# Graph-attention kernel: biases of neighbouring projections as two 32-row products in different row groups, and all bias parts in one tile

## Chip, cores and metric

The kernel runs on one NeuronCore of a Trainium2 chip. The metric is device time in microseconds (us), as the median of the runs; the profile describes one execution, and its span reaches from the first to the last instruction.

## The reference

One pre-norm graph-attention layer with B = 16 batches, N = 1024 nodes, D = 512 channels, and 8 heads of 64 channels, all in fp32. The adjacency matrix is sparse and shared by the batches; a node attends only to the nodes it is linked to.

```python
h = jnp.maximum(_layernorm(x, axis=-1), 0.0)
q = (h @ Wq + bq).reshape(b, n, H, HD)
k = (h @ Wk + bk).reshape(b, n, H, HD)
v = (h @ Wv + bv).reshape(b, n, H, HD)
scores = jnp.einsum('bihd,bjhd->bhij', q, k) / jnp.sqrt(jnp.float32(HD))
scores = scores + jnp.where(adj == 0, -1e9, 0.0)[None, None, :, :]
weights = jax.nn.softmax(scores, axis=-1)
out = x + jnp.einsum('bhij,bjhd->bihd', weights, v).reshape(b, n, H * HD)
```

The setup sets the three bias vectors to zero, but the kernel computes with whatever they hold.

## The kernel before, in words

**Tiles.** The nodes are sorted by degree once, at the start, and each batch is handled as 8 tiles of 128 nodes in that order. For each tile n the kernel loads the rows of x (`load_x`), takes layer-norm statistics on VectorE (`stats`, `variance`, `shift`, with `power` on GpSimd), normalises on ScalarE (`norm`, L644), turns the tile over with four TensorE transposes (`flip`, L651), and copies the result to SBUF on ScalarE (`unflip`, L656). Then come three projections of that tile by TensorE: K and V (`proj_kv`, evicted from PSUM by ScalarE at L672 into `kvt` and stored to a table `kv` in DRAM) and Q (`queries`, which stays in PSUM in tile `pq` until VectorE has multiplied it with the gathered keys at L895).

**One projection.** `project` (L658 to L661) issues five matrix products into one PSUM tile of 128x512. First the bias: a bf16 matrix product of `chosen` (128x128, rows 0, 64 and 96 ones, the rest zeros) with `bias[name]` (128x512, whose rows 0, 64 and 96 hold the bias as a sum of three bf16 parts). Then, for four chunks of 128 input channels, the fp32 product of the turned tile with the weights; each of these four appears as two instructions in the profile, so that a projection is one bias instruction and eight product instructions. There are 384 projections: 128 each of K, V and Q.

**Attention.** A unit is a tile (or a part of one) with up to four neighbours per node. GpSimd gathers rows of K and V from the `kv` table with indirect DMAs (`gather`, L885), VectorE multiplies with q and sums over each head (`multiply` L895, `score` L899), ScalarE takes the exponential and weights V (`exponent` L903, `weigh_s` L921), VectorE and GpSimd add the neighbours up (`fold` L926), and TensorE adds up for the tiles that are not folded fully (`add_up` L944). Output rows leave by indirect DMA (`put_out`, L988). A batch's first gather needs all eight tiles of that batch's K and V in the table, so the projections of the next batch run beside the attention of the present one.

**Order.** Nothing is scheduled by the compiler. `plan_of` lists every step with an engine, an assumed length, a place and what it depends on, and simulates the five engines; the order that comes out is the order in which the steps are written, and each engine takes its own instructions in that order. A projection is planned with 3.70 us (K, V) or 3.66 us (Q). PSUM has two buffers for K and V (`pkv`) and two for Q (`q`).

**Bias at the start.** `load_b` (L514) issues three small DMAs per bias from SyncE, nine in all, one into each of rows 0, 64 and 96 of a zeroed fp32 scratch area, behind the loads of two x tiles and of Wk and ahead of the loads of the other x tiles and of adj. `round` (L518) casts to bf16 on ScalarE, `remain` (L522) subtracts on GpSimd what the cast has kept, and each bias goes through round, remain, round, remain, round: nine casts and six subtractions. A K projection waits only for K's last cast, and so on.

Of the kernel before, what the change touches and what calls it, by code (L numbers as in the profile page):

```python
# [45 lines left out]

UNITS = (
    (7, 0, 2),
    (6, 0, 3),
    (5, 0, 3),  # L50
    (4, 0, 4),
    (3, 0, 3),
    (3, 3, 2),
    (2, 0, 3),
    (2, 3, 3),
    (1, 0, 4),
    (1, 4, 4),
    (0, 0, 4),
    (-1, 0, 4),
    (0, 4, 4),  # L60
    (0, 8, 3),
)
SHARES = (7, 6, 5, 4)
DIRECT = (7, 6, 5, 4, 3, 2, 1)
LAST_ORDER = (10, 11, 12, 13, 8, 9, 6, 7, 4, 5, 3, 2, 1, 0)
LAST_DIRECT = (7,)
POOL_FOLDS = (2, 3, 8, 9, 11)
UMAX = max(n for _, _, n in UNITS)
SLOTS = sum(n for _, _, n in UNITS) + len(CAPS) + 1
NU = len(UNITS)  # L70
NT = len(CAPS)
BY_VECTOR = {2: 1, 3: 0, 4: 1}
ONE_MORE = (6,)
BY_VECTOR_LAST = {2: 1, 3: 1, 4: 1}
# [97 lines left out]
def plan_of(B):  # L172
# [15 lines left out]
    for k, load in enumerate(loads):  # L188
        uses = [("x", load[1])] if load[0] == "load_x" else []
        add(load, "SP", 0.9 if load[0] == "load_b" else 0.2, -90 + k, uses=uses, delay=4.6, moves=size[load[0]])  # L190
    for j in range(3):
        for k, name in enumerate(names):
            place = -70 + 4 * k + j
            add(("round", name, j), "ACT", 0.58, place, [("remain", name, j - 1) if j else ("load_b", name)])
            if j < 2:
                add(("remain", name, j), "POOL", 1.3, place, [("round", name, j)])
    for t in range(NT):
# [40 lines left out]
    for n in range(-NT, tiles):  # L238
        b, j = divmod(n, NT)
        ahead = 0 if n >= 0 else 60 if n < 4 - NT else 19.47 - 1.3 * j  # L240
        p = (b - 1) * NU + j * rate if b > 0 else j * rate - 20.77 if b == 0 else 1.5 * j - 42.92
        if n >= 0:
            known = [("perm_of",)] if b == 0 else []
            add(("load_x", n), "POOL", 1.35, p - 5.47, known, [("x", n)], delay=4.5, moves=0.75)
        if b:
            add(("stats", n), "DVE", 0.84, p - ahead - 4.00, [("load_x", n)], [("x", n)])
        m, k, size = group_of(n)
        if b and k == size - 1:
            add(("variance", m), "DVE", 0.33, p - ahead - 5.38, [("stats", n - k) for k in range(size)])
            add(("power", m), "POOL", 1.1, p - ahead - 4.87, [("variance", m)])  # L250
            add(("shift", m), "DVE", 0.37, p - ahead - 4.29, [("power", m)])
        add(("norm", n), "ACT", 0.76, p - 6.38, [("shift", m) if b else ("load_x", n)], [("x", n), ("h", n)], delay=0.00)
        add(("flip", n), "PE", 0.62, p - 3.43, [("norm", n)], [("h", n), ("pht", n)])
        add(("unflip", n), "ACT", 0.53, p - 2.57, [("flip", n)], [("pht", n), ("hT", n)])
        if b == 0:
            continue
        for w in range(2):
            e = p - -0.51 + 0.3 * w + (1.41 if n < 3 - NT and w else 0.0)
            ready = [("unflip", n)]
            if n < 0:  # L260
                ready += [("round", "kv"[w], 2), ("load_w", "kv"[w])]
            add(("proj_kv", n, w), "PE", 3.70, e, ready, [("hT", n), ("pkv", n, w)])
            add(("evict_kv", n, w), "ACT", 0.53, e - 0.99, [("proj_kv", n, w)], [("pkv", n, w), ("kvt", n)])
        ready = [("evict_kv", n, w) for w in range(2)]
        if n >= 0:
            add(("store_kv", n), "SP", 0.1, p, ready, [("kvt", n)], delay=2.5, moves=1.5)
        else:
            add(("store_kv", n), "POOL", 1.35, p, ready + [("ranks",)] + ([("store_kv", n - 1)] if n > -NT else []), [("kvt", n)], delay=2.5, moves=1.5)
# [3 lines left out]
    for k in range(units):  # L272
# [4 lines left out]
        t, _, count = UNITS[u]  # L277
        n = b * NT + NT - 1 - t
        q = ("q", b, t)
        if q not in q_of:  # L280
            p = i - 2.12
            if t >= 0:
                ready = [("unflip", n)] + ([("round", "q", 2), ("load_w", "q")] if b == 0 else [])
                add(("queries", b, t), "PE", 3.66, p, ready, [("hT", n), q])
                if t == 0:
                    add(("copy_q", b), "ACT", 0.57, p + 0.5, [("queries", b, 0)], [q, ("q0", b)])
            else:
                add(("queries", b, t), "PE", 0.9, p, [("copy_q", b)], [q, ("q0", b)])
# [26 lines left out]
        for n in folds(b, B, t, count):  # L315
            on_pool = n[1] == 1 and u in POOL_FOLDS
            add(("fold", k, *n), "POOL" if on_pool else "DVE", 1.4 if on_pool else 0.45 * n[1] + 0.35, i + 0.90, weighed, [g], delay=1.67 if on_pool else 0.15)
# [14 lines left out]
        if u == parts[-1]:  # L332
            n = b * NT + NT - 1 - home
            by = ("DVE", 0.75) if residual_by_vector(b, B, home) else ("POOL", 1.5)
# [41 lines left out]


def by_vector(b, B, u):

    count = UNITS[u][2]  # L380
    return BY_VECTOR[count] + (u in ONE_MORE) if b < B - 1 else BY_VECTOR_LAST[count]

# [18 lines left out]
def main_path(tc, x, adj, Wq, bq, Wk, bk, Wv, bv, out, sums, cover):  # L401
# [10 lines left out]
    with ExitStack() as ctx:  # L412
# [35 lines left out]
        matrices = dict(k=Wk, v=Wv, q=Wq)  # L448
        rest = {name: scratch[:, 0, ts(k, H * HD)] if k < 2 else scratch[:, 1, : H * HD] for k, name in enumerate(names)}
        nc.gpsimd.memset(scratch[:, 0:2, :], 0.0)  # L450
# [11 lines left out]

        starts = (0, 64, 96)
        chosen = const.tile([P, P], BF16, tag="chosen", name="chosen")
        nc.gpsimd.memset(chosen, 0.0)
        for start in starts:
            nc.gpsimd.memset(chosen[start : start + 1, :], 1.0)
        minus_half = const.tile([P, 1], F32, tag="mhalf", name="minus_half")
# [27 lines left out]
        nc.gpsimd.tensor_copy(before["told"][:, :, own], place)  # L496
        bias = {name: const.tile([P, H * HD], BF16, tag="b" + name, name=f"b{name}_parts") for name in names}

# [15 lines left out]
        def load_b(name):  # L514
            for start in starts:
                nc.sync.dma_start(rest[name][start : start + 1, :], vectors[name].rearrange("(o n) -> o n", o=1))

        def round(name, j):  # L518
            rows = slice(starts[j], P)
            nc.scalar.copy(bias[name][rows, :], rest[name][rows, :])  # L520

        def remain(name, j):  # L522
            rows = slice(starts[j + 1], P)
            nc.gpsimd.tensor_tensor(rest[name][rows, :], rest[name][rows, :], bias[name][rows, :], ALU.subtract)

# [72 lines left out]
        def tile_at(n):  # L598


            return (n // NT, NT - 1 - n % NT) if n >= 0 else ("first", n + NT)

# [54 lines left out]

        def project(pt, name, n):  # L658
            nc.tensor.matmul(pt, chosen, bias[name], start=True, stop=False)  # L659
            for c in range(DC):  # L660
                nc.tensor.matmul(pt, HT[n][:, c, :], W[name][:, c, :], start=False, stop=(c == DC - 1))  # L661

        def proj_kv(n, j):
            b, t = tile_at(n)
            PT[n, j] = ps_kv.tile([P, D], F32, tag="pkv", name=f"p{'kv'[j]}_{b}_{t}")
            project(PT[n, j], "kv"[j], n)

# [199 lines left out]
        def queries(b, t):  # L867
            Q[b, t] = ps_q.tile([P, D], F32, tag="q", name=f"pq_{b}_{t}")
            if t >= 0:
                project(Q[b, t], "q", b * NT + NT - 1 - t)  # L870
            else:
# [51 lines left out]
        def fold(i, first, n):  # L923
            v = G[i][:, :, 1, :]
            engine = nc.gpsimd if n == 1 and i % NU in POOL_FOLDS else nc.vector
            engine.tensor_tensor(v[:, 0:n], v[:, 0:n], v[:, first : first + n], ALU.add)  # L926
# [55 lines left out]
        def residual(b, t):  # L982
            rows = X[b * NT + NT - 1 - t]
            add = G.pop(b * NU + parts_of(t)[0])[:, 0, 1, :] if shares_in(b, B, t) else O.pop((b, t))
            (nc.vector if residual_by_vector(b, B, t) else nc.gpsimd).tensor_tensor(rows, rows, add, ALU.add)  # L985

        def put_out(b, t):
            nc.gpsimd.indirect_dma_start(  # L988
                out=out_rows, out_offset=on(ap=perm[:, t : t + 1], axis=0), in_=X.pop(b * NT + NT - 1 - t)[:], in_offset=None,
                element_offset=b * N * D,  # L990
            )

        do = (
            zeros, load_adj, load_w, load_b, round, remain, degree, no_diagonal, keys, flip_row, copy_row, rank_of, ranks, ends, list_of,
            tell, spread, collect, others, perm_of, spots, long_rows, long_blocks, longest, count_pieces, first_piece, owners, flip_owners, copy_owners, list_pieces, pieces, slots, load_x, stats, variance, power, shift, norm, flip, unflip, proj_kv, evict_kv, store_kv,
# [3 lines left out]
        do = {f.__name__: f for f in do}  # L999
        for name, *args in plan_of(B):  # L1000
            do[name](*args)
# [186 lines left out]
```

## Time and profile before

| what | value |
|---|---|
| median of 3 runs | 1742.09 us (1739.52 to 1748.52) |
| span of the profiled execution | 1721.4 us |
| granted TensorE clock, mean | 0.981 |
| TensorE products, busy | 1601.7 us, 93% of the span, 4295 instructions |
| VectorE, ScalarE, GpSimd, busy | 87%, 86%, 73% of the span |
| mean DMA rate | 309 GB/s |

The profiled execution's own time is known only as its span. The median lies 20.7 us above that span: start and end of the launch, which the profile does not cover, and the difference from run to run. In the lines of the profile, PE is TensorE's products, PEld its weight loads (which run beside products), DVE is VectorE, ACT ScalarE, POOL GpSimd and SP SyncE; an instruction's end on PE is modelled, its start is recorded. A form such as 128*128 is the part of the array used, rows by columns; `128x512 bf16` is the operand. L659 is line 659 of the kernel.

### The profile page before, as it was taken

The numbers are of one execution on the slowest core, as the hardware profiler recorded it, in microseconds if no ns is written. First come the engines' busy times: TensorE is split into PE (matmuls) and PEld (weight loads), VectorE is DVE, ScalarE is ACT, GpSimd is POOL, SyncE is SP. The second block draws the span as 40 slices with busy tenths as digits, with TensorE's granted clock in tenths as the row PEclk, the third lists the DMA queues.
The fourth block names the chain that finished last, engine by engine and source line by source line (L and its number), as shares of the span: only waits on it lengthen the run. The fifth ranks groups of instructions, "written<-read, shape, count | busy, mean of one in ns | idle before, by whom it ended". The sixth has DMA issues, their size and how long they took to land.

```text
span 1721.4 us, 19566 instructions
## 1 busy us (share of the span) xinstructions
PE 1601.7 (93%) x4295; PEld 740.1 (43%) x4295; DVE 1506.2 (87%) x1921; ACT 1479.7 (86%) x5484; POOL 1264.2 (73%) x1161
## 2 busy tenths in 40 slices
PE   6979999999999999999999999999999999999896
PEld 3434444444444444444444444444444444444332
DVE  6789889898989989899998889989888998988896
ACT  5249989898998989899898989989898997979895
POOL 4757777787877778777877778778687777867654
PEclk9989999999999999999999999999999999999998
DMA  6397889899898989989898898889989888988893
GB/s 235 122 319 269 313 309 348 315 336 331 305 327 303 360 309 331 325 306 326 306 358 320 308 338 301 324 311 338 337 317 329 298 318 312 336 329 290 299 356 141
DMA packets 150741, 531.73 MB, mean 309 GB/s; under 512 B 19916, under 2 KB 19916, under 8 KB 150616
## 3 DMA queue, kind: packets, MB, share of 16 engines
q0 software_dynamic: 109840, 390.70, 64.4%
q1 hardware_dynamic: 40776, 139.71, 21.4%
q8 instruction: 36, 0.59, 0.1%
q14 instruction: 89, 0.73, 0.1%
HBM read 429.51 MB, written 100.82 MB: 308 GB/s over the span
## 4 chain that ended last, share of the span: by engine, by line
PE 74%; DMA 9%; DVE 3%; POOL 2%; ACT 1%; issue 1%; DVEq 0%; POOLq 0%; ACTq 0%
PE pv L661 22%; PE pk L661 22%; PE pq L661 20%; DMA g<-kv,index 8%; PE acc L944 3%; DVE g L895 2%; PE pht L651 2%; PE pv L659 1%; PE pk L659 1%; PE pq L659 1%; POOL g L885 1%; DMA kv<-kvt 1%; ACT hT L656 0%; ACT h L644 0%; DMA out_dram<-x,perm 0%
## 5 line engine op out<-in xcount | busy, mean ns | idle before, releaser
L921 ACT ACTIVATE g<-g,weights 128x64 f32<-128x64 f32 x4696 | 1155.8, 338 | 15.1 <-DVE weights L908 14.3
L885 POOL DMA_INDIRECT g<-kv,index x608 | 631.3, 1038 | 225.7 <-issue 144.5
L895 DVE TENSOR_TENSOR g<-g,pq 128x1536 f32<-128x1536 f32 (+2 forms) x208 | 388.1, 1871 | 101.6 <-DMA g<-kv,index 73.7
L661 PE MATMUL pq<-wq,hT 128*128 128x512 f32 x1024 | 470.8, 603 | 0.0
L661 PE MATMUL pk<-wk,hT 128*128 128x512 f32 x960 | 431.5, 592 | 0.0
L661 PE MATMUL pv<-wv,hT 128*128 128x512 f32 x960 | 431.5, 592 | 0.0
L899 DVE TENSOR_REDUCE weights<-g 128x32 f32<-128x2048 f32 (+2 forms) x224 | 424.1, 1893 | 0.6
L661 PEld LDWEIGHTS pq<-wq,hT 128*128 128x128 f32 x1024 | 198.1, 193 | 273.9 <-issue 270.1
L926 DVE TENSOR_TENSOR g<-g 128x512 f32<-128x512 f32 (+1 forms) x301 | 257.7, 860 | 27.6 <-ACT g L921 27.2
L661 PEld LDWEIGHTS pv<-wv,hT 128*128 128x128 f32 x960 | 182.4, 190 | 215.1 <-issue 212.0
L661 PEld LDWEIGHTS pk<-wk,hT 128*128 128x128 f32 x960 | 182.4, 190 | 205.5 <-issue 202.0
L609 POOL DMA_INDIRECT x<-in_x_dram,perm x128 | 148.8, 1162 | 39.9 <-issue 33.6
L988 POOL DMA_INDIRECT out_dram<-x,perm x128 | 133.7, 1045 | 50.9 <-issue 19.9
L926 POOL TENSOR_TENSOR g<-g 128x512 f32<-128x512 f32 x90 | 118.9, 1321 | 67.5 <-DVE g L926 58.6
L915 DVE TENSOR_TENSOR g<-g,weights 128x512 f32<-128x512 f32 x149 | 124.3, 834 | 2.1 <-ACT weights L903 1.8
L644 ACT ACTIVATE h<-x,shift,rstd 128x512 f32<-128x512 f32 x120 | 94.5, 812 | 28.7 <-issue 14.7
L903 ACT ACTIVATE weights<-weights 128x32 f32<-128x32 f32 (+2 forms) x224 | 49.7, 222 | 71.9 <-DVE weights L899 71.8
L985 POOL TENSOR_TENSOR x<-x,o 128x512 f32<-128x512 f32 x67 | 89.3, 1333 | 11.5 <-DVE o L976 7.8
L944 PE MATMUL acc<-g,ident 128*128 128x512 f32 x170 | 86.4, 622 | 9.0 <-DMA g<-kv,index 5.4
L659 PE MATMUL pq<-bq_parts,chosen 128*128 128x512 bf16 x128 | 48.8, 382 | 47.9 <-DVE g L895 47.9
L651 PE MATMUL pht<-ident,h 128*128 128x128 f32 x512 | 73.8, 276 | 18.5 <-ACT hT L656 16.5
L651 PEld LDWEIGHTS pht<-ident,h 128*128 128x128 f32 x512 | 60.6, 142 | 64.7 <-issue 33.9
(231 smaller groups left out, 1147.5 us busy)
## 6 DMA issues: line engine op xcount, KB each, us to landing
g<-kv SPq DMA_DIRECT2D x128, 512.0 KB
kv<-kvt SPq DMA_DIRECT2D x120, 512.0 KB
g<-kv,index POOLq DMA_INDIRECT x608, 6.8
adj<-in_adj_dram SPq DMA_DIRECT2D x8, 512.0 KB
x_first<-in_x_dram SPq DMA_DIRECT2D x8, 256.0 KB
x<-in_x_dram,perm POOLq DMA_INDIRECT x128, 6.3
out_dram<-x,perm POOLq DMA_INDIRECT x128, 5.5
wk<-in_L_gnn_Wk_dram SPq DMA_DIRECT2D x1, 1024.0 KB
```

Of the source, the lines that this page charges most:

```text
L609: nc.gpsimd.indirect_dma_start(out=X[n][:], out_offset=None, in_=x_rows, in_offset=on(ap=perm[:, t : t + 1], axis=0), element_offset=b * N * D
L651: nc.tensor.transpose(PH[n][:, c, :], hn[:, ts(c, P)], ident)
L659: nc.tensor.matmul(pt, chosen, bias[name], start=True, stop=False)
L661: nc.tensor.matmul(pt, HT[n][:, c, :], W[name][:, c, :], start=False, stop=(c == DC - 1))
L885: nc.gpsimd.indirect_dma_start(out=G[i][:, s].rearrange("p j d -> p (j d)"), out_offset=None, in_=KV[b % len(KV)][:], in_offset=on(ap=inde ...
L895: nc.vector.tensor_tensor(k, k, Q[b, t][:, None, :].to_broadcast([P, count, D]), ALU.mult)
L899: nc.vector.tensor_reduce(weights[:, w, :], heads(G[i][:, :count, 0, :]), AX.X, ALU.add)
L915: nc.vector.tensor_tensor(v, v, own.to_broadcast([P, n, H, HD]), ALU.mult)
L921: nc.scalar.activation(v[:, h, :], v[:, h, :], AF.Identity, scale=weights[:, c + s, h : h + 1])
L926: engine.tensor_tensor(v[:, 0:n], v[:, 0:n], v[:, first : first + n], ALU.add)
L944: nc.tensor.matmul(ACC[b, home], owner_t if t < 0 else ident, v[:, s, :], start=(u == parts_of(home)[0] and s == 0), stop=(u == parts_of(h ...
L988: nc.gpsimd.indirect_dma_start(out=out_rows, out_offset=on(ap=perm[:, t : t + 1], axis=0), in_=X.pop(b * NT + NT - 1 - t)[:], in_offset=No ...
```

## The change

It does the following, and leaves the rest of the computation as it is.

- **One bias tile.** The three biases lie in one 128x512 bf16 tile, in four groups of 32 rows, in the order k, v, q, q. The first three rows of a group hold the three parts of its bias, the other 29 are zero.
- **Loading.** Each group is filled by one DMA that writes the vector into three rows: four DMAs in place of nine.
- **Splitting.** `parts_at` makes two columns of ones and zeros on VectorE (rows from which the second and third part count), with two reductions and two small operations. The split then runs once for all biases: three ScalarE steps (the first two with a scale column) and two GpSimd subtractions, over all 128 rows. All projections now wait for the last of these.
- **Products.** `bias_places` goes through TensorE's steps in the planned order. Where two projections follow each other directly, and are not K after K or V after V, they form a pair: the first takes its bias at its end, the second at its beginning, so that the two bias products stand side by side. Each is a 32-row product with all-one weights from another group of 32 rows. A projection without such a neighbour keeps a 128-row bias product at its beginning, with a weight matrix (`chosen_of`) that has ones in its own group's rows.
- **Names.** Units, orders and shares are now named by tile and first neighbour rather than by number (`TILES`, `PARTS`, `LAST_TILES`, `POOL_FOLDS`, `ONE_MORE`). The values come out the same as before.

The core of the diff:

```diff
-            add(("round", name, j), "ACT", 0.58, place, [("remain", name, j - 1) if j else ("load_b", name)])
-            if j < 2:
-                add(("remain", name, j), "POOL", 1.3, place, [("round", name, j)])
+    add(("parts_at",), "DVE", 0.5, -70)
     for j in range(3):
+        known = [("remain", j - 1)] if j else [("parts_at",)] + [("load_b", name) for name in names]
+        add(("round", j), "ACT", 0.58, -70 + j, known)
+        if j < 2:
+            add(("remain", j), "POOL", 1.3, -70 + j, [("round", j)])
...
+def bias_places(order):
+    on_pe = ("proj_kv", "queries", "flip", "add_up", "pass_on", "flip_row", "first_piece", "flip_owners", "list_pieces")
+    ops = [op for op in order if op[0] in on_pe]
+    name = lambda op: None if op[0] not in ("proj_kv", "queries") or op[2] == -1 else "q" if op[0] == "queries" else "kv"[op[2]]
+    at = {}
+    for one, two in zip(ops, ops[1:]):
+        if one in at or name(one) is None or name(two) is None:
+            continue
+        g, h = GROUPS.index(name(one)), GROUPS.index(name(two))
+        if g == h:
+            if GROUPS.count(name(one)) == 1:
+                continue
+            h = GROUPS.index(name(one), g + 1)
+        at[one], at[two] = (False, g), (True, h)
+    return at
...
-        starts = (0, 64, 96)
         chosen = const.tile([P, P], BF16, tag="chosen", name="chosen")
-        nc.gpsimd.memset(chosen, 0.0)
-        for start in starts:
-            nc.gpsimd.memset(chosen[start : start + 1, :], 1.0)
+        nc.gpsimd.memset(chosen, 1.0)
+        chosen_of = const.tile([P, len(names), P], BF16, tag="chosen_of", name="chosen_of")
+        nc.gpsimd.memset(chosen_of, 0.0)
+        for g in range(len(names)):
+            nc.gpsimd.memset(chosen_of[32 * g : 32 * g + 32, g, :], 1.0)
...
         def load_b(name):
-            for start in starts:
-                nc.sync.dma_start(rest[name][start : start + 1, :], vectors[name].rearrange("(o n) -> o n", o=1))
+            vec = vectors[name]
+            rows = bass.AP(tensor=vec.tensor, offset=vec.offset, ap=[[0, 3], [1, H * HD]])
+            for g, owner_name in enumerate(GROUPS):
+                if name == owner_name:
+                    nc.sync.dma_start(rest[32 * g : 32 * g + 3, :], rows)
+
+        def parts_at():
+            ends_at = [once.tile([P, 1], F32, tag=f"ends{j}", name=f"ends_at_{j}") for j in range(2)]
+            for j in range(2):
+                nc.vector.tensor_reduce(ends_at[j], ident.rearrange("p (g r) -> p g r", r=32)[:, :, j], AX.X, ALU.add)
+            nc.vector.tensor_scalar(later[0], ends_at[0], -1.0, 1.0, op0=ALU.mult, op1=ALU.add)
+            nc.vector.tensor_tensor(later[1], later[0], ends_at[1], ALU.subtract)
+
+        def round(j):
+            if j < 2:
+                nc.scalar.activation(part, rest, AF.Identity, scale=later[j])
+            else:
+                nc.scalar.copy(bias, rest)
+
+        def remain(j):
+            nc.gpsimd.tensor_tensor(rest, rest, part, ALU.subtract)
...
-        def project(pt, name, n):
-            nc.tensor.matmul(pt, chosen, bias[name], start=True, stop=False)
+        def project(pt, name, n, op):
+            ahead, g = bias_at.get(op, (True, None))
+            rows = slice(0, P) if g is None else slice(32 * g, 32 * g + 32)
+            ones = chosen_of[:, GROUPS.index(name), :] if g is None else chosen[rows, :]
+            if ahead:
+                nc.tensor.matmul(pt, ones, bias[rows, :], start=True, stop=False)
             for c in range(DC):
-                nc.tensor.matmul(pt, HT[n][:, c, :], W[name][:, c, :], start=False, stop=(c == DC - 1))
+                nc.tensor.matmul(pt, HT[n][:, c, :], W[name][:, c, :], start=(c == 0 and not ahead), stop=(c == DC - 1 and ahead))
+            if not ahead:
+                nc.tensor.matmul(pt, ones, bias[rows, :], start=False, stop=True)
```

## The prediction

> **What bounds the kernel now.** I read first the page's busy times and the shares of the chain that ended last (its engines, then its lines), to see which engine sets the end.
>
> ```profile
> PE 1601.7 (93%) x4295; PEld 740.1 (43%) x4295; DVE 1506.2 (87%) x1921; ACT 1479.7 (86%) x5484; POOL 1264.2 (73%) x1161
> ...
> PE 74%; DMA 9%; DVE 3%; POOL 2%; ACT 1%; issue 1%; DVEq 0%; POOLq 0%; ACTq 0%
> PE pv L661 22%; PE pk L661 22%; PE pq L661 20%; DMA g<-kv,index 8%; PE acc L944 3%; DVE g L895 2%; PE pht L651 2%; PE pv L659 1%; PE pk L659 1%; PE pq L659 1%; POOL g L885 1%; DMA kv<-kvt 1%; ACT hT L656 0%; ACT h L644 0%; DMA out_dram<-x,perm 0%
> ```
>
> TensorE's projections are most of the chain; the bias products (L659) are in it with some 1% for each of pq, pk and pv. The one sizeable other link is the gather, which the list of the chain shows as 8 to 9 us once a batch. A stretch of 100 us, about one batch, says how much room the others have (columns: busy us and count for PE, PEld, DVE, ACT, POOL, then clock, DMA share, GB/s):
>
> ```profile
> 400.00:500.00 100.00, 95.74 (x260) 44.30 (x259) 90.30 (x108) 91.52 (x343) 76.61 (x69) 1.00 0.90 329
> ```
>
> VectorE, ScalarE and the DMA engines have 8 to 10% left, and TensorE nothing but the waits. These are TensorE's two largest in the list of waits (total us, times, longest):
>
> ```profile
> PE pq L659 <- DVE g L895: 47.9, 28, 4.1
> PE pht L651 <- ACT hT L656: 16.5, 17, 1.0
> ```
>
> The first comes twice a batch, where a batch begins: q's PSUM buffers are full until the first gathers land. So a batch is TensorE's row of products plus this fixed gap. The price of a bias product is read in the timeline of PE (start, us, then the instructions merged), and of its weight load in that of PEld:
>
> ```profile
> 833.40 0.38 PE L659 MATMUL pq<-bq_parts,chosen 128*128 128x512 bf16 x1
> 833.62 3.60 PE L661 MATMUL pq<-wq,hT 128*128 128x512 f32 x8
> 837.05 0.38 PE L659 MATMUL pk<-bk_parts,chosen 128*128 128x512 bf16 x1
> 837.26 3.60 PE L661 MATMUL pk<-wk,hT 128*128 128x512 f32 x8
> 840.70 0.38 PE L659 MATMUL pv<-bv_parts,chosen 128*128 128x512 bf16 x1
> ```
>
> ```profile
> 836.19 0.19 PEld L661 LDWEIGHTS pq<-wq,hT 128*128 128x128 f32 x1 [0.24 <-issue]
> 836.62 0.10 PEld L659 LDWEIGHTS <-chosen 128*128 128x128 bf16 x1 [0.24 <-issue]
> 837.05 0.41 PEld L661 LDWEIGHTS pk<-wk,hT 128*128 128x128 f32 x2 [0.33 <-issue]
> ```
>
> A projection takes 837.05 - 833.40 = 3.65 us from start to start. Its bias holds the stream for about 0.216 us (833.40 to 833.62; over the whole trace these gaps are 0.21 or 0.22), and the eight products for 3.65 - 0.216 = 3.43, or 0.429 each. The record of 0.379 is longer than the 0.216 by 0.163, as the product's 0.592 is by 0.163 over 0.429: a tail that the next instruction overlaps. Both loads, 0.098 and 0.190 us, start with the product ahead of theirs and hide under it.
>
> **What the Trainium skill says.** (1) "TensorEngine Tiling (Array Packing)", Key Properties: tiles of the array work independently, but a change of tiling mode drains TensorE. Every form in the trace of before but the last check's is 128*128, so no change of row mode is in it, and it neither agrees nor disagrees. (2) "TensorE: Matmul & The Clock Gate", Part 3, The mechanism: products in different row groups start about 4 ns apart, and loads are pulled ahead where row groups don't conflict. The trace shows loads pulled ahead with full rows only. (3) The same page, Part 2, LDWEIGHTS: a load's time goes by columns, not rows, so a 32-row load should cost the 0.098 us that the trace has for 128 rows.
>
> **The change part by part.** *Pairs.* Going through TensorE's steps of the trace in order, I paired direct neighbours by the change's rule: 170 pairs (95 k-v, 30 v-q, 15 q-k, 15 k-q, 14 q-q, 1 v-k) and 44 single projections, 384 in all. About 11 pairs fall in each batch. The order is the plan's, and its costs for projections stay, so I keep this number.
>
> *The stream.* A pair's two bias products took 2 x 0.216 = 0.432. Side by side they take 0.216 + 0.004 = 0.220, if nothing else is added: 0.212 saved, and 170 x 0.212 = 36.0 us. The one large unknown is the change of mode, twice per pair (128 rows to 32, and back). No row here has it. Bounds: below, nothing (the two stream as any other two do; a gain beyond the saved stream is excluded, since one of the two must still be streamed). Above, at each change the full tail of 0.163 stands free and neither load can be pulled ahead: 2 x 0.163 + 0.098 + 0.190 = 0.614 per pair, or 0.614 - 0.212 = 0.402 lost, 170 x 0.402 = 68 us. I take the lower end: the loads of two disjoint row groups don't conflict with one another and fit under the last product (0.196 of 0.429 us), and the next full load (0.190) fits under the pair (0.220). Break-even is 0.212 / 2 = 0.106 per change.
>
> *How much reaches the end.* The 14 q-q pairs stand where a batch begins, next to the waits for L895; what they save goes into those waits. 156 x 0.212 = 33.1 us are left. The neighbours have 8 to 10% room for a batch that is 2% shorter, but gathers and q's buffers will be late more often; I take off 15%, an estimate, to 28 us. Full carry would be 36, half 18.
>
> *Second bias, PSUM.* The second product of a pair claims its PSUM buffer directly behind the first's; the buffers alternate as before, and no wait stands inside a pair in the trace, so nothing. If the second should wait, the pair falls apart, and the first one's eviction on ScalarE, already released, doesn't suffer. The first's eviction comes after its bias rather than its last product, and the bias ahead is gone: nothing.
>
> *Single projections.* `chosen_of` has the same shape as `chosen`, so 0.216 as before.
>
> *The start.* The rows of SP's queue and the first of VectorE's work on adj:
>
> ```profile
> 2.63 0.88 SPq L516 DMA_DIRECT2D scratch<-in_L_gnn_bk_dram  x3
> 3.56 1.38 SPq L516 DMA_DIRECT2D scratch<-in_L_gnn_bv_dram  x3
> 4.98 5.17 SPq L516 DMA_DIRECT2D scratch<-in_L_gnn_bq_dram  x3
> 10.19 0.83 SPq L607 DMA_DIRECT2D x_first<-in_x_dram  x2
> ...
> 16.52 1.22 DVE L530 TENSOR_SCALAR_CACHE_REDUCE junk<-adj 128x1024 f32<-128x1024 f32 x1 [0.55 <-DMA adj<-in_adj_dram]
> ```
>
> Nine issues held SP from 2.63 to 10.15, with the x and adj loads queued behind. Four at some 0.3 us would end near 4. The data still queue behind 1.5 MB of x and Wk, and the stretch from 0 to 20 us has a DMA share of 0.66, so adj can come up to some 3 us earlier, not 6. VectorE runs without a gap from 16.52 through the degrees to 28.6, so this would move; but TensorE, busy with K and V from 16 to 85 us, doesn't need it all. I take 1.5 us gained, bounds -0.5 and +3. Six casts (6 x 0.61) and four subtractions (4 x 1.15) go; they lay beside TensorE's work, except that GpSimd's power step at 17.13 stood behind a subtraction for 1.2 us. Added: four small VectorE operations (0.7 us, about 0.17 each as its other small ones) ahead of the statistics, covered because GpSimd takes these up only at 12.74; without that cover, 0.7. Memsets on GpSimd, net some 0.35 us, lie before its idle time from 7.1 to 11.5. The new wait of all projections for all biases: GpSimd's first subtraction, with the power step and so the first transposes (14.56) queued behind it, now waits for four loads rather than three; they come behind Wk alike, and I put it at 0.3, within the bounds.
>
> *Sum.* Against the profiled execution: 1721.4 - 28 - 1.5 = 1692 of span. The median is 20.7 above the span, which the change doesn't touch: 1742.1 - 29.5, rounded, 1713.
>
> **The rivals.**
> *A, partial drain.* Only the array's depth empties. By the same page's Part 2 (drain, 128 cycles at 2.4 GHz), an estimate of 0.053 per change: 0.212 - 0.106 = 0.106 saved, 18 us, with 0.85 carried 15, less 1.5: 1726. At 0.106 nothing is left: 1741. For it: the page's sentence. Against: that no trace shows a mode.
> *B, full drain, slower.* Each change waits for the tail: 2 x 0.163 - 0.212 = 0.114 lost per pair, 19.4 us; at 0.9 (the rest falls into waits) 17.5, less 1.5: 1758. With one load exposed as well, 0.212 to 0.304 lost: 32 to 47 us, up to 1787. It decides from 0.106 per change on. For it: the skill's sentence, and that TensorE has no slack to hide it. Against: the tail is modelled, not recorded.
> *C, drain and both loads exposed.* 68 us x 0.9 - 1.5: 1802.
> *D, the change doesn't do what it says.* The products stream one after the other: 1741, by the start alone.
>
> **How the numbers follow.** Forecast 0.42 (1704 to 1724 by full and by poor carry), A 0.16, B 0.20, C 0.18, D 0.04. A measurement of this kernel can tell about 0.5%, 8.7 us: 1733.4 to 1750.8 count as the same. Faster: the forecast and half of A, 0.50. Same: the rest of A, D and a little of B, 0.13. Slower: 0.37. Cases of both signs hold most of the chance; the forecast's own range is 1704 to 1724. The range leaves out C and the thin ends: 1704 to 1790.
>
> **What would show it.** In the timeline of PE: two 32-row products whose starts lie a few ns apart, the next full product 0.22 us behind them, and two projections in 7.08 us rather than 7.30. A gap of more than 0.43 between the last product's start and the pair's, or of more than 0.22 after it, is a drain; a PEld row of L659 or L661 that begins only when PE stands still is an exposed load. PE's wait for L895 should rise by a few us, and adj should land a little sooner. I am wrong if the two gaps add up to over 0.21 us, or if VectorE takes over as the end of a batch.

## The result, and the profile after

The changed kernel is slower, by a little under 1%: a ratio of 1.0092 to before (95% interval 1.0064 to 1.0119), medians 1761.98 against 1744.27 us. A second measurement on another chip gave 1.0061 (1.0040 to 1.0081). The forecast was 1713 us, the rival with a full drain 1758.

Chips differ here, with medians of before from 1725 to 1754 us, so that below only ratios to before on the same chip are compared.

The page of after has these lines in place of those shown of before:

```profile
PE 1625.7 (92%) x4295; PEld 708.1 (40%) x4295; DVE 1516.5 (86%) x1925; ACT 1478.7 (84%) x5478; POOL 1265.9 (72%) x1158
...
PE 76%; DMA 6%; issue 3%; ACT 2%; DVE 2%; POOL 0%; another core or an unknown queue 0%; DVEq 0%; POOLq 0%; ACTq 0%
```

TensorE is still most of the chain. The timeline of PE after shows a K and a V projection that form a pair, in the middle of a batch:

```profile
442.39 3.60 PE L701 MATMUL pk<-wk,hT 128*128 128x512 f32 x8
445.93 0.38 PE L703 MATMUL pk<-bias_parts,chosen 32*128 32x512 bf16 x1
445.93 0.39 PE L699 MATMUL pv<-bias_parts,chosen 32*128 32x512 bf16 x1
446.25 3.70 PE L701 MATMUL pv<-wv,hT 128*128 128x512 f32 x8
449.78 0.38 PE L685 MATMUL pht<-ident,h 128*128 128x128 f32 x2
```

The two 32-row products start together, as they were meant to (in all 170 pairs the records of the two starts are 3 or 4 ns apart). But the pair takes 449.78 - 442.39 = 7.39 us, where two projections took 2 x 3.65 = 7.30 before. Sixteen products of 0.429 are 6.86; the bias part is about 0.52 us rather than 0.43, and so it is in all 170 pairs. The timeline of PEld says where it goes:

```profile
444.97 0.19 PEld L701 LDWEIGHTS pk<-wk,hT 128*128 128x128 f32 x1 [0.24 <-issue]
445.92 0.09 PEld L703 LDWEIGHTS <-chosen 32*128 32x128 bf16 x1 [0.76 <-issue]
445.93 0.09 PEld L699 LDWEIGHTS <-chosen 32*128 32x128 bf16 x1
446.24 0.30 PEld L701 LDWEIGHTS pv<-wv,hT 128*128 128x128 f32 x2 [0.23 <-issue]
```

Before, a bias's load started with the last product, which would be at 445.39 here (442.39 + 7 x 0.429). Now it starts at 445.92, 0.1 us after that product's stream has ended at 445.82. The two loads run side by side, 0.09 us with no stream; then the two products stream for 0.22, to 446.24. Only there does the next full load begin, and the second product of V comes 0.53 us after the first, not 0.43: another 0.10 in the open. So 0.10 of drain (the time between the end of the full stream and the small load), 0.09 of load, 0.22 of stream and 0.10 of load, some 0.52 in all. The sum is measured; the split is a reading, since the profile records the starts of loads and products and not the stream itself.

The two pages differ by 43 us of span, far more than the two medians do. 16 us of this lie before the first full batch: the first `p_more` product, which ends the first batch's sums, starts at 199.33 us in the trace of before and at 215.21 after. The first experiment shows that this comes with the kernel before too.

### The profile page after: what moved, and what is told of

The parts are those of the page before. It is cut to its first block, busy times and chain, and to the rows that moved or that the text cites. A ratio compares the mean times of both kernels' runs of the same rounds, so it can differ in the third digit from the quotient of the medians.

```text
span 1764.8 us, 19553 instructions
## 1 busy us (share of the span) xinstructions
PE 1625.7 (92%) x4295; PEld 708.1 (40%) x4295; DVE 1516.5 (86%) x1925; ACT 1478.7 (84%) x5478; POOL 1265.9 (72%) x1158
## 4 chain that ended last, share of the span: by engine, by line
PE 76%; DMA 6%; issue 3%; ACT 2%; DVE 2%; POOL 0%; another core or an unknown queue 0%; DVEq 0%; POOLq 0%; ACTq 0%
PE pv L701 24%; PE pk L701 23%; PE pq L701 20%; DMA g<-kv,index 5%; PE acc L986 3%; PE pht L685 2%; PE pk L703 2%; DVE g L937 2%; ACT g L963 1%; DMA kv<-kvt 1%; PE pq L699 1%; PE pv L703 1%; DMA out_dram<-x,perm 0%; PE pq L703 0%; DVE weights L941 0%
## 5 line engine op out<-in xcount | busy, mean ns | idle before, releaser
L701 PE MATMUL pq<-wq,hT 128*128 128x512 f32 x1024 | 482.6, 615 | 0.0
L701 PE MATMUL pv<-wv,hT 128*128 128x512 f32 x960 | 440.9, 602 | 0.0
L701 PEld LDWEIGHTS pq<-wq,hT 128*128 128x128 f32 x1024 | 193.4, 196 | 273.0 <-issue 271.4
L701 PEld LDWEIGHTS pk<-wk,hT 128*128 128x128 f32 x960 | 178.8, 190 | 211.5 <-issue 210.7
L701 PEld LDWEIGHTS pv<-wv,hT 128*128 128x128 f32 x960 | 175.0, 190 | 207.0 <-issue 206.0
L957 DVE TENSOR_TENSOR g<-g,weights 128x512 f32<-128x512 f32 x149 | 131.9, 885 | 7.1 <-remote 4.9
L690 ACT COPY hT<-pht 128x512 f32<-128x512 f32 x128 | 73.2, 574 | 21.2 <-PE pht L685 15.5
```

Source lines behind the costliest of these rows:

```text
L957: nc.vector.tensor_tensor(v, v, own.to_broadcast([P, n, H, HD]), ALU.mult)
```

## Experiments

The theory (M): a change of row mode, that is from products on all 128 rows of the array to products on 32 or 64 of them, costs TensorE time, some 0.31 us for the way there and back, against 0.21 saved by streaming side by side. Rivals: the start of the kernel (S) and the order of bias and products (O). For how much of TensorE's time reaches the end there are two theories: the clock (K: after a longer wait TensorE is granted half its clock for some us, which takes time back) and the other engines (V: VectorE, ScalarE or the gathers are full themselves and set the pace).

**before_again.** The kernel before; no edit.

> The kernel before, unchanged, for a second trace. The profiled execution of before had a span of 1721.4 us, while runs of the changed kernel lie only 1.7 us above their span, so the profiled execution was some 20 us shorter than the runs of before. Theory S (a stall at the start that comes and goes): VectorE's search for the longest rows, which took 15 us without a gap in the trace of before and 29 us with gaps of up to 2.5 us in the trace after, shows the gaps here too, and the first p_more product comes near 215 us rather than 199. Rival: the stall belongs to the changed kernel, this trace is as the first one, with p_more near 199 us and a span near 1721. Time about 1744 in either case.

Ratio 0.9989 (0.9975 to 1.0004). In its trace the first `p_more` starts at 217.84 us, and VectorE's search for the longest rows has gaps of the kind that the trace after has:

```profile
85.70 0.09 DVE L759 MATCH_VALUE_LOAD adj_long<-adj_long 128x8 f32 x1 [0.98 <-DVE adj_long L758]
...
87.15 0.09 DVE L759 MATCH_VALUE_LOAD adj_long<-adj_long 128x8 f32 x1 [0.65 <-DVE adj_long L758]
...
89.27 0.09 DVE L759 MATCH_VALUE_LOAD adj_long<-adj_long 128x8 f32 x1 [0.98 <-DVE adj_long L758]
```

So both kernels have them. What the gaps come from wasn't settled; on the chip of the last experiments, where before takes 1725 us, they are hardly there (first `p_more` at 201.5).

**packed_only.** Packed tile, no pairs.

```diff
-        bias_at = bias_places(order)
+        bias_at = {}
```

> The changed kernel's packed bias tile, loads and split, but no pairs: every projection takes a 128-row bias product at its beginning. Theory M (the loss is the change of row mode, 170 times): 1741 to 1745, as before or a little less, since the start's loads come 2 us sooner. Rival S (the loss is made at the start, by the new order of loads and casts): 1758 to 1764, as the changed kernel.

0.9986 (0.9969 to 1.0003). The start's part of the change is worth nothing that can be measured; S falls.

**pairs_full.** Pairs in the changed order, with 128-row products.

```diff
-            rows = slice(0, P) if g is None else slice(32 * g, 32 * g + 32)
-            ones = chosen_of[:, GROUPS.index(name), :] if g is None else chosen[rows, :]
+            rows = slice(0, P)
+            ones = chosen_of[:, GROUPS.index(name), :]
```

> The changed kernel with its pairs, the first one's bias at its end and the second's at its beginning, but both as 128-row products. Theory M: no change of mode, 0.432 us for two bias products as before, 1741 to 1745. Rival O (the order costs: a bias behind the products delays evictions, or takes the cover from the next load): 1755 to 1764.

0.9974 (0.9956 to 0.9991). The order costs nothing (the interval even lies just below 1); O falls. What costs is the 32-row form.

**lone32.** Every bias as one 32-row product.

```diff
-        bias_at = bias_places(order)
+        bias_at = {op: (True, GROUPS.index("q" if op[0] == "queries" else "kv"[op[2]])) for op in order if op[0] == "proj_kv" or op[0] == "queries" and op[2] >= 0}
```

> The changed kernel without pairs, but every projection's bias is a single 32-row product at its beginning: 768 changes of mode in place of 340. Theory M: a bias then takes 0.525 us (0.11 of drain, 0.09 of load, 0.22 of stream, 0.10 of load, as read in the trace after) rather than 0.216, 384 x 0.309 = 119 us, of which nine tenths reach the end: 1744 + 107 = 1851. Rivals O and S: no more than the changed kernel, 1762; rival M2 (only the meeting of two row groups costs): 1744.

1.0217 (1.0189 to 1.0245), some 38 us. The local price is as expected; a projection takes 453.21 - 449.26 = 3.95 us, 0.30 more than before:

```profile
449.26 0.39 PE L699 MATMUL pk<-bias_parts,chosen 32*128 32x512 bf16 x1
449.58 3.70 PE L701 MATMUL pk<-wk,hT 128*128 128x512 f32 x8
453.21 0.39 PE L699 MATMUL pv<-bias_parts,chosen 32*128 32x512 bf16 x1
```

So the change of mode costs the same with one product as with two. But of 384 x 0.30 = 115 us only a third reached the end, not nine tenths.

**same_group.** Both products of a pair in one row group.

```diff
-        at[one], at[two] = (False, g), (True, h)
+        at[one], at[two] = (False, g), (True, g)
```

> The changed kernel, but the second bias product of a pair uses the first one's row group (and so adds the first one's bias; this leaves the second projection's own bias out). The two can't stream side by side. Theory M (side by side saves 0.212 us, the two changes of mode take 0.31): a pair takes 0.525 + 0.216 = 0.741 us rather than 0.432, 170 x 0.309 = 52 us, 1790 to 1796. Rival (the two row groups never ran side by side, and the record's starts only look so): as the changed kernel, 1762.

1.0088 (1.0053 to 1.0124). Locally the expectation held: the starts are 0.23 apart, and the pair takes 453.01 - 445.41 = 7.60 us.

```profile
445.41 3.60 PE L701 MATMUL pq<-wq,hT 128*128 128x512 f32 x8
448.94 0.39 PE L703 MATMUL pq<-bias_parts,chosen 32*128 32x512 bf16 x1
449.17 0.37 PE L699 MATMUL pk<-bias_parts,chosen 32*128 32x512 bf16 x1
449.47 3.70 PE L701 MATMUL pk<-wk,hT 128*128 128x512 f32 x8
453.01 0.59 PE L701 MATMUL pv<-wv,hT 128*128 128x512 f32 x1
```

Streaming side by side is thus real and worth 7.60 - 7.39 = 0.21 us. The time at the end missed: the ratio is that of the changed kernel (1.0061 and 1.0092, on other chips), though TensorE has 51 us more to do and not 15.

**rows64.** Groups in the order k, q, v, q; a pair uses the two halves of the array, with 64-row products.

```diff
...
-            rows = slice(0, P) if g is None else slice(32 * g, 32 * g + 32)
-            ones = chosen_of[:, GROUPS.index(name), :] if g is None else chosen[rows, :]
+            rows = slice(0, P) if g is None else slice(64 * (g // 2), 64 * (g // 2) + 64)
+            ones = chosen_of[:, GROUPS.index(name), :] if g is None else chosen_of[rows, g, :]
```

> The changed kernel with 64-row products: the bias tile's groups lie in the order k, q, v, q, and a pair's products use the upper and the lower half of the array, with weights that pick one group out of the half. Theory M, the change of row mode as such costs: 1758 to 1766 as with 32 rows. Rival: the cost grows as the row groups get smaller, so that halves are cheaper: 1744 to 1752.

1.0036 (0.9996 to 1.0075), too wide to choose. The trace does: a pair with 64-row products takes 7.39 us too (447.88 to 455.27). Halves are no cheaper than quarters.

**no_bias.** No bias products.

```diff
-            if ahead:
-                nc.tensor.matmul(pt, ones, bias[rows, :], start=True, stop=False)
...
-            if not ahead:
-                nc.tensor.matmul(pt, ones, bias[rows, :], start=False, stop=True)
...
```

> The changed kernel's loads and split, but no projection adds a bias at all (the bias products are left out). It takes 384 x 0.216 = 83 us from TensorE. Theory of the prediction (85% of TensorE's time reaches the end): 1744 - 70 = 1674. Rival (VectorE, ScalarE or the gathers, each at 90% of a batch, take over): 1700 or more.

0.9911 (0.9879 to 0.9943): 16 us of 83. The rival holds, and the 85% of the prediction falls.

**no_k_bias.** K's product alone left out of the kernel before.

```diff
-            nc.tensor.matmul(pt, chosen, bias[name], start=True, stop=False)
+            if name != "k":
+                nc.tensor.matmul(pt, chosen, bias[name], start=True, stop=False)
...
```

> The kernel before without K's bias product. A bias of K adds the same number to all scores of a node and head, and the softmax takes it out again, so the layer's result keeps its value. It takes 128 x 0.216 = 27.6 us from TensorE without any change of mode. If 85% reaches the end: 1744 - 23 = 1721. Rival (the neighbours take over after the first few us): 1732 or more.

1.0025 (0.9992 to 1.0058): of 27.6 us nothing that can be measured arrives. The granted clock of these runs has a median of 0.958, against 0.974 for before on the same chip.

The trace of no_bias shows where such time goes. TensorE's wait where a batch begins has grown to 5.88 us, and the eight products behind it take 5.68 us rather than the usual 3.6. In the stretches (columns as before: PE, PEld, DVE, ACT, POOL, clock, DMA) of 25 us around that place and of the 65 us behind it, the first has a clock of 0.86, and the second ScalarE at 64.65 of 65 us:

```profile
530.00 5.68 PE L699 MATMUL pq<-wq,hT 128*128 128x512 f32 x8 [5.88 <-DVE g L933]
```

```profile
514.60:539.60 25.00, 18.81 (x47) 8.52 (x46) 17.91 (x26) 15.77 (x58) 15.90 (x15) 0.86 0.87 334
539.60:604.60 65.00, 64.00 (x167) 29.38 (x166) 59.33 (x70) 64.65 (x249) 50.60 (x47) 1.00 0.89 319
```

The kernel before does it too, in some batches. In before_again one wait of 3.79 us is followed by slow products (5.96 us for eight), one of 1.63 us by quick ones:

```profile
533.98 0.59 PE L659 MATMUL pq<-bq_parts,chosen 128*128 128x512 bf16 x1 [3.79 <-DVE g L895]
534.36 5.96 PE L661 MATMUL pq<-wq,hT 128*128 128x512 f32 x8
...
635.01 0.38 PE L659 MATMUL pq<-bq_parts,chosen 128*128 128x512 bf16 x1 [1.63 <-DVE g L895]
635.23 3.59 PE L661 MATMUL pq<-wq,hT 128*128 128x512 f32 x8
...
838.67 0.38 PE L659 MATMUL pq<-bq_parts,chosen 128*128 128x512 bf16 x1 [2.02 <-issue]
838.89 5.29 PE L661 MATMUL pq<-wq,hT 128*128 128x512 f32 x8
```

The length of one wait doesn't settle it: the last two lines show slow products after 2.02 us, and in the trace of after a wait of 3.47 us is followed by quick ones:

```profile
1456.87 0.38 PE L699 MATMUL pq<-bias_parts,chosen_of 128*128 128x512 bf16 x1 [3.47 <-DVE g L937]
1457.09 3.59 PE L701 MATMUL pq<-wq,hT 128*128 128x512 f32 x8
```

In the batches of before_again the clock is at half for 3.41 us six times and for 6.83 us twice.

**after_again and plain_dose.** The changed kernel once more, and beside it the changed order with 128-row products and some plain TensorE time more in each pair, planned as 0.092 us:

```diff
...
                 nc.tensor.matmul(pt, ones, bias[rows, :], start=True, stop=False)
+                if g is not None:
+                    nc.tensor.matmul(pt[:, :220], ones, bias[rows, :220], start=False, stop=False)
```

> The changed kernel, unchanged, timed beside the next three on one chip. Theory M with full carry (170 x 0.093 = 15.8 us of TensorE time, all of which reaches the end): a ratio of 1.009 to before. Rival (part of it goes into TensorE's wait at the start of a batch, as most of the 51 us of the same-group kernel did): 1.003 to 1.006.

> The pairs in the changed order, both as 128-row products, and in each pair one more 128-row product over 220 columns, 0.092 us of stream (it adds the second bias once more in these columns, so the computation is another). This is the changed kernel's added TensorE time, 170 x 0.092 = 15.6 us, without any change of mode. Theory M (a change of mode is nothing but TensorE time): as the changed kernel beside it, within 0.3%. Rival (a change of mode also delays something that more TensorE time doesn't): as before, 0.997 to 1.001.

1.0061 (1.0040 to 1.0081) and 1.0047 (1.0029 to 1.0065) on one chip. In the trace of plain_dose a pair takes 446.55 - 439.14 = 7.41 us, so that the dose came out as 0.11 us or 19 us in all, where the changed kernel has 15. Plain TensorE time of about this size costs the same within the intervals: no other delay by a change of mode is seen, and one of less than some 0.3% can't be excluded.

**keep_warm and warm_no_k.** Products of zero weights to shorten TensorE's wait, in the kernel before and in no_k_bias:

```diff
...
+            if u == parts_of(0)[-1] and b < B - 1:
+                for _ in range(2):
+                    nc.tensor.matmul(ACC[b, home], nothing, W["k"][:, 0, :], start=False, stop=False)
             for s in range(count):
```

> The kernel before, with two products of an all-zero weight matrix added into the last tile's sum at the end of each batch but the last (they add zero), 1.7 us of TensorE time where it then waits for the first gathers. Theory K ([...]the granted clock falls to half for the next few us, and the batch takes 103 us rather than 100.5): no such batch is left, 1.3 us less per batch, 0.989 to 0.993. Rival (the long batches come from elsewhere, and the clock only follows): 1.000 or more.

> The same two products, and no bias product for K (27.6 us less of TensorE time; a bias of K shifts all scores of a node and head alike and leaves the softmax as it is). Theory K: what no_k_bias gave back by a clock of 0.97 in every batch is kept, and the ratio is 0.980 to 0.990, below that of the zero products alone. Rival (VectorE and ScalarE, full in the body of a batch, allow no more): as the zero products alone, within 0.3%.

1.0012 (0.9991 to 1.0034) and 1.0041 (1.0020 to 1.0062). Both miss what K had forecast, but they don't test K: in the trace of keep_warm the zero products stand behind the wait (a wait of 4.12 us ends at 534.47, the zero products start at 541.01). They show that such products gain nothing there.

**warm2, warm2_no_k, warm2_no_bias.** The zero products one unit earlier, ahead of the wait; two, three and four of them.

```diff
...
+            if u == parts_of(0)[2] and b < B - 1:
...
```

> The kernel before with two products of an all-zero weight matrix (they add zero), now ahead of TensorE's wait at the start of each next batch: 1.7 us of filling, so that no wait is over 2.5 us. Theory K: no batch with a clock below 1.00, about 100.6 us for each, 0.988 to 0.994. Theory V: the clock rises, but the batches stay at some 101.5, 0.998 to 1.003.

> No bias product for K (softmax takes such a bias out again) and three zero products ahead of the wait. Theory K: 0.980 to 0.990, clock back to 1.00 in the batches. Theory V: 0.995 to 1.003 in spite of the clock.

> No bias products at all (left out), and four zero products ahead of the wait. Theory K: without the 3.2 us per batch that the clock took, 97.5 us per batch and 0.962 to 0.970. Theory V: as without the zero products, 100 us per batch or a little less, 0.985 to 0.993.

0.9936 (0.9918 to 0.9954), 0.9929 (0.9902 to 0.9956) and 0.9881 (0.9848 to 0.9915). Now they fill the gap, and the wait is 0.74 us here (two batches still have one of 2.6 and of 3.2 us):

```profile
508.12 1.88 PE L947 MATMUL acc<-wk,nothing 128*128 128x512 f32 x4
509.83 1.02 PE L949 MATMUL acc<-g,ident 128*128 128x512 f32 x2
511.59 0.38 PE L661 MATMUL pq<-bq_parts,chosen 128*128 128x512 bf16 x1 [0.74 <-DVE g L897]
511.81 3.59 PE L663 MATMUL pq<-wq,hT 128*128 128x512 f32 x8
```

TensorE does 1.7 us more per batch and the kernel is faster, as K had forecast (0.988 to 0.994): K holds in the kernel before. The size fits too: on this chip the median granted clock is 0.988 against 0.981 for before, and 0.007 of 1720 us is 12 us, an estimate from above, since a low clock costs nothing where TensorE is idle; 11 us were gained. warm2 beats both kernels. At the large dose V holds: without any bias, and with the gap filled, the gain grows only from 0.9 to 1.2%, not to the 3 to 4% that K alone had expected. And there the clock didn't fully return (11 of 14 batches still below 1.00), and TensorE then waits for ScalarE's `norm` in the body, 22.0 us in all and up to 4.2 at once, so that the two theories aren't wholly apart. warm2_no_k lies between the ranges of K and V and is not to be told from warm2, though no batch of its trace has a low clock: without K's products nothing more arrives even then.

## Why the prediction was wrong

The table puts the runs in order of the TensorE time that they add to before (instructions times the local price). A batch reaches from one `p_more` product to the next, 14 per trace; TensorE's wait is the sum of its waits in that stretch. The last three columns of each row are of one execution, and the rows come from three chips.

| kernel | TensorE time, us | ratio | wait per batch, us | batches with clock below 1.00 | mean batch, us |
|---|---|---|---|---|---|
| no_bias | -83 | 0.9911 | 6.5 | 14 | 100.7 |
| no_k_bias | -28 | 1.0025 | 5.3 | 14 | 102.0 |
| before_again | 0 | 0.9989 | 4.6 | 8 | 101.8 |
| after_again | +15 | 1.0061 | 4.4 | 5 | 102.2 |
| same_group | +51 | 1.0088 | 2.6 | 3 | 102.7 |
| lone32 | +115 | 1.0217 | 1.2 | 0 | 104.6 |

*The mode change.* The step that failed is "I take the lower end: the loads ... fit under the last product ... and the next full load ... fits under the pair". Neither load is pulled ahead over a change of mode. The term for the change of mode was put at 0 and measures some 0.30 per pair (0.10 drain, 0.09 and 0.10 of load), so a pair loses 0.09 us instead of gaining 0.21; 170 x 0.09 = 15 us. The stated break-even, 0.106 per change, was passed: it came to 0.15. The 32-row load itself took 0.09 us, where the prediction had 0.098. The Trainium skill's sentence on tiling modes ("TensorEngine Tiling (Array Packing)", Key Properties), used only for rivals, described the case; the trace puts 0.10 us of drain beside it, on the way in; on the way out no gap is left between stream and load. That products in different row groups start about 4 ns apart, as the Trainium skill also says ("TensorE: Matmul & The Clock Gate", Part 3), held, with 3 or 4 ns in the records.

*The rival B* named the right side and nearly the size (0.114 per pair), but by another sum: two full tails and hidden loads, where the runs show one shorter drain and loads in the open. Its 1758 us agrees with the measured ratio (1.0092 x 1742 = 1758) in part by luck. Rival C had the loads in the open, but with two full tails.

*How much reaches the end.* "I take off 15%" failed as well, and by these runs would have spoiled the forecast even with free mode changes: 83 us taken away gave 16, 28 gave none. TensorE's idle time was read as a fixed gap; it isn't. Less TensorE work makes the wait at the start of a batch longer, and the lower clock behind it then takes back part of it in every batch; and in the body of a batch ScalarE is nearly full beside TensorE. The mean of 91.52 of 100 us, in the stretch that the prediction shows, hid this. Cut in two, the trace of before has ScalarE at 19.11 of 25 us where a batch begins and at 63.42 of 65 behind it (the fourth busy time in each line):

```profile
400.60:425.60 25.00, 21.73 (x64) 10.43 (x63) 20.14 (x32) 19.11 (x69) 17.02 (x16) 1.00 0.89 337
425.60:490.60 65.00, 64.01 (x173) 29.50 (x172) 60.16 (x68) 63.42 (x242) 52.51 (x49) 1.00 0.90 324
```

That ScalarE holds the body is read from such lines and from TensorE's waits; no run here makes ScalarE faster, so it isn't shown. More TensorE work in turn fills the gap and spares the clock, so that 115 us cost 38.

The traces give the account per batch. Half of the time that TensorE is busy at half clock is lost: 1.1 us in before_again, 2.4 in no_k_bias, 2.6 in no_bias and none in lone32. Products, wait and this loss together change by 7.2 - 3.4 - 1.1 = 2.7 us in lone32, where the mean batch grew by 2.8; by -1.7 + 0.7 + 1.3 = 0.3 in no_k_bias, where it grew by 0.2; and by -5.2 + 1.9 + 1.5 = -1.8 in no_bias, where it fell by 1.1.

Of the 15 us of the change, 11 arrived in after_again (7 to 14 by the interval) and 16 in the first measurement (11 to 21).

*The start.* SP's four bias loads are issued by 3.89 us and adj's first operation on VectorE comes at 13.24 rather than 16.52, as forecast ("some 3 us earlier"); what reaches the end is below what packed_only can tell.

*The number of pairs*, 170 and 44 single projections, was exact. *Single projections, order, second bias*: nothing, as forecast (pairs_full).

*What lies around the span.* The 20.7 us between span and median were no launch time: the later runs lie some 1.7 us above their spans. The profiled execution of before was shorter than the median, by its start and by fewer batches with a low clock. With some 1723 us and a clock of 0.981 it is like before on the chip of the last experiments (1725 us, 0.981), and may have been taken on such a chip; the record doesn't say. This shifted no difference, but the page showed a kernel with fewer long waits than the other trace of before has (5 and 8 batches with a low clock).

Open: where VectorE's gaps at the start come from, and why one chip doesn't have them; how much of the floor of about 100 us per batch is ScalarE's, and how much the gathers'; and why the first 15 us of added TensorE time cost nearly as much at the end as the 51 us of same_group.

## What to carry to other kernels

Small products in separate row groups do stream side by side, but going from full rows to a row group and back costs about 0.3 us here, two thirds of it for loads that aren't pulled ahead over the change and the rest for a drain; it pays only when more than that is saved per visit. No run here had more than two products per visit. Before time is taken from the busiest engine, split the stretch into body and gap: an engine that is full in the body beside it, and a clock that drops in a longer gap, can keep all of it. Where TensorE waits for 2 us or more and the products behind the wait are slow, filling the wait can be worth more than shortening the work around it.

## What the runs showed of the hardware that wasn't expected

- A change from 128 rows to 32 or to 64 and back has one price: a pair takes 7.39 us with either. A lone 32-row product of 512 columns takes 0.52 us, where a 128-row one takes 0.22.
- After a wait of 3.79 us eight fp32 products took 5.96 us, after one of 2.02 us 5.29, after 1.63 us 3.59; but after one of 3.47 us, in another trace, also 3.59. Products with all-zero weights in the wait were enough to keep the clock (1 of 14 batches below 1.00 in warm2).
